# Fused two-layer transformer block on one core: x kept turned through the second half, queries and keys by column quarters, and each sample's own adapters in the linear layer

## Chip, core and metric

The kernel runs on one core of a Trainium2 chip. The metric is the device time of one launch in microseconds (us), as the median of several runs. A profiled execution gives the trace. PE is TensorE, DVE is VectorE, ACT is ScalarE, POOL is GpSimd, and SP is the queue that issues most plain DMAs.

## What is computed

64 samples of 32 tokens with 256 features, all f32, go through two layers of two residual blocks each. Several weights are picked by a per-sample index.

```python
x = x + L0_attn(L0_cond(x, idx1))       # first half
x = x + L0_ffn(L0_cond2(x, idx2))       # gated MLP with rank-16 adapters, then a ternary gated FFN
# L1_cond: H = x @ W.T;  xa = x @ A[idx3].T;  H + (xa @ B[idx3].T) * scalings[idx3]
# L1_attn: qkv = h @ W_qkv + b_qkv; 16 heads of 16; rotation of 4 of the 16; causal softmax; @ W_dense + b_dense
x = x + L1_attn(L1_cond(x, idx3))
# L1_cond2: x @ W[idx4] + b[idx4];  L1_ffn: both sides rounded to 8-bit steps, silu(gate) * up, down
x = x + L1_ffn(L1_cond2(x, idx4))
```

A and B hold 8 adapters of rank 16. W of L1_cond2 has 16 experts of 256 x 256.

## The kernel before

The 2048 tokens are eight chunks of 256 (8 samples). xq[ch] holds a chunk as two groups of 128 tokens in the partitions and 256 features in the columns. The order of instructions on each engine is the order in which the Python code lists them; nothing reorders them later.

The first half is 32 steps (4 groups of heads by 8 chunks). turn(n) mixes stages of the steps n-2 to n+1: projections and rotation (L700 on PE, L711 and L712 on DVE, L714 and L715 on POOL), scores (L810), weigh (qe, L857 on POOL), turn_qe (L871), f2 (L931 on POOL) and more. After each turn, one piece of tabulate() is listed: SP copies adapter matrices in DRAM into a layout in which one indirect gather fetches an adapter. prepare() quantizes weights of the later FFNs. load_weights brings each group's weights, load_mlp those of the second half.

The second half is turn2(n) for n from 0 to 7, and then drain(). In turn2(n), chunk n goes through gated MLP (adapters_in L401, adapters_spread L417, gate_up L436, gate_up_adapters L450, down_adapters L466, down L482), ternary FFN (ffn_up L507, ffn_down L526) and linear layer (linear_in, linear_adapters L543, linear L555 and L560). Chunk n-1 goes through attention (qkv L1098, turn_qk L1136, attn_scores L1159, attn_exp, attn_weights with the transpose L1193, attn_values L1208, attn_out L1230). Chunk n-2 goes through experts (experts_in, run_experts L1271) and the quantized FFN (turn_y, quant_up L1301, quant_h on DVE, turn_h L1325, quant_down L1341). PE works with features in the partitions for most products, so a chunk's x is turned on PE (L342, four transposes, copied out by ACT at L347) in tokens_in, linear_in and experts_in, while the residual sums are made on xq. [...]

In the linear layer before, one product with all 8 adapters side by side gives 128 rows, a mask m6 keeps the rows of each sample's own adapter, and one product with all B follows. linear_in also adds the dense bias db to xq on POOL (L537). Queries, keys and values come from one weight, qkvw, as 384 columns at a time with tokens in the partitions; turn_qk then turns queries and keys on PE in eight transposes, ACT scales the queries and DVE spreads the keys into kb.

POOL issues the indirect gathers: fetch (experts, 10 a chunk), fetch_in, fetch_out, fetch_down (adapters of the next chunk). gather copies an index column on DVE first (L366). [...] A tile is waited for where the order needs it: kb before scores, u (adapters_spread) before gate_up_adapters, h of quant_h before turn_h.

## Time and profile before

| What | Value |
|---|---|
| Median of 3 runs (lowest to highest) | 1463.49 us (1462.98 to 1463.92) |
| Profiled execution: time, span | 1462.34 us, 1460.6 us |
| Mean granted TensorE clock | 0.988 |
| First half; second half's turns; drain | to about 839; to about 1393; to 1460.6 us |
| Busy: PE, DVE, ACT, POOL | 97%, 57%, 42%, 35% of the span |

A row of the profile reads: line, engine, operation, output and inputs by the program's names, shape, count, busy us and mean ns of one, and then the idle time just before with what ended it. In a timeline the first two numbers are start and duration in us. Busy matmuls overlap, so the distance of two starts says what a step takes. An f32 matmul of the program is two records.

### The profile page before, as it was taken

How to read it: one execution, taken by the hardware profiler on the slowest of the kernel's cores; microseconds unless marked ns; L12 is line 12 of the kernel's file. 1: busy time of each engine (PE TensorE's matmuls, PEld its weight loads, DVE VectorE, ACT ScalarE, POOL GpSimd, SP SyncE). 2: the span in 40 equal slices, each digit the busy share in tenths (PEclk: the TensorE clock that was granted, in tenths of full speed). 3: DMA queues.
4: the chain of work that ended last, by engine and by line, in shares of the span. 5: the costliest groups of instructions: out<-in, count | busy, mean ns of one | idle time of the engine just before them, and what ended most of it. 6: DMA issues, size and time to landing. Idle time of an engine off the chain costs nothing.

```text
span 1460.6 us, 37036 instructions
## 1 busy us (share of the span) xinstructions
PE 1411.5 (97%) x15496; PEld 1082.4 (74%) x15496; DVE 827.1 (57%) x1899; ACT 617.0 (42%) x2014; POOL 514.4 (35%) x586
## 2 busy tenths in 40 slices
PE   5899999999999999999999999999999999999997
PEld 3666777777777777667767878788887878787865
DVE  2566677776768676667565224363636263534555
ACT  1355575656566575746566312121312121222121
POOL 3433243333424243324354243333252515152130
PEclk9999999999999999999999999999999999999999
DMA  6201010100111000100001222122221212121120
GB/s 182 55 2 66 2 30 31 34 2 12 33 39 41 9 9 12 46 2 1 13 16 50 72 79 74 52 73 59 58 75 55 78 38 84 41 73 46 43 77 18
DMA packets 61503, 65.14 MB, mean 45 GB/s; under 512 B 34901, under 2 KB 48853, under 8 KB 61337
## 3 DMA queue, kind: packets, MB, share of 16 engines
q0 software_dynamic: 13312, 35.93, 8.8%
q1 hardware_dynamic: 44824, 22.33, 5.6%
q10 hardware_dynamic: 3200, 4.52, 1.0%
q8 instruction: 122, 2.00, 0.6%
q14 instruction: 45, 0.36, 0.1%
HBM read 60.66 MB, written 3.93 MB: 44 GB/s over the span
## 4 chain that ended last, share of the span: by engine, by line
PE 92%; DMA 2%; DVE 2%; issue 2%; ACT 1%; SPq 1%; POOL 0%; DVEq 0%; POOLq 0%; ACTq 0%
PE ps L700 16%; PE ps L731 15%; PE ps L968 8%; PE ps L436 8%; PE ps L507 5%; PE ps L1301 5%; PE ps L482 3%; PE ps L1341 3%; PE ps L1098 3%; PE ps L526 3%; PE ps L913 2%; PE ps L810 2%; PE ps L450 2%; PE ps L953 2%; PE ps L888 1%
## 5 line engine op out<-in xcount | busy, mean ns | idle before, releaser
L714 POOL TENSOR_TENSOR qT<-ra,rb 128x256 f32<-128x256 f32 x64 | 46.5, 727 | 365.0 <-DVE rb L712 365.0
L922 ACT ACTIVATE sq<-ps 128x128 f32<-128x128 f32 x256 | 70.9, 277 | 213.9 <-PE ps L913 206.8
L368 POOL DMA_INDIRECT we<-in_ew,at x64 | 61.4, 960 | 255.5 <-DVE at L366 170.6
L968 PE MATMUL ps<-wo,ogT 128*128 128x256 f32 x512 | 123.3, 396 | 6.7 <-DVE aT L817 6.7
L700 PE MATMUL ps<-hsT,wq 128*128 128x256 f32 x512 | 126.5, 391 | 0.0
L700 PE MATMUL ps<-hsT,wk 128*128 128x256 f32 x512 | 121.5, 380 | 0.0
L711 DVE TENSOR_TENSOR ra<-ps,ct 128x512 f32<-128x512 f32 x128 | 87.6, 684 | 49.1 <-PE ps L700 44.1
L731 PE MATMUL ps<-wv,hsT 128*128 128x512 f32 x256 | 115.2, 593 | 0.0
L731 PE MATMUL ps<-wg,hsT 128*128 128x512 f32 x256 | 115.1, 592 | 0.0
L968 PEld LDWEIGHTS ps<-wo,ogT 128*128 128x128 f32 x512 | 97.8, 196 | 21.9 <-DVE aT L817 7.3
L700 PEld LDWEIGHTS ps<-hsT,wq 128*128 128x128 f32 x512 | 95.6, 192 | 18.3 <-issue 6.0
L794 DVE RECIPROCAL enz<-ps 128x256 f32<-128x256 f32 x64 | 107.5, 1721 | 1.5 <-PE ps L785 1.5
L700 PEld LDWEIGHTS ps<-hsT,wk 128*128 128x128 f32 x512 | 97.9, 191 | 13.4
L931 POOL TENSOR_TENSOR f<-f,mhalf 128x8 f32<-128x8 f32 x32 | 52.9, 1652 | 132.3 <-DVE f L929 132.3
L731 PEld LDWEIGHTS ps<-wg,hsT 128*128 128x128 f32 x256 | 48.7, 190 | 61.2 <-issue 54.0
L712 DVE TENSOR_TENSOR rb<-ps,ct 128x512 f32<-128x512 f32 x128 | 87.2, 681 | 0.0
L848 ACT ACTIVATE qv<-ok,nmx 128x64 f32<-128x64 f32 x256 | 84.9, 335 | 1.9 <-DVE nmx L844 1.9
L731 PEld LDWEIGHTS ps<-wv,hsT 128*128 128x128 f32 x256 | 48.6, 190 | 47.5 <-issue 45.9
L1301 PE MATMUL ps<-guT,y3T 128*128 128x352 f32 x256 | 79.6, 465 | 1.2 <-ACT y3T L347 1.2
L817 DVE SCALAR_TENSOR_TENSOR aT<-ps,ct 128x256 f32<-128x256 f32 x64 | 24.2, 419 | 86.8 <-PE ps L810 86.8
L458 DVE TENSOR_TENSOR hT<-ps,sg 128x256 f32<-128x256 f32 x64 | 24.3, 420 | 83.5 <-ACT sg L457 83.5
L507 PE MATMUL ps<-yT,f 128*128 128x256 f32 x320 | 71.2, 382 | 0.2 <-ACT yT L493 0.2
(225 smaller groups left out, 2985.3 us busy)
## 6 DMA issues: line engine op xcount, KB each, us to landing
x<-in_x SPq DMA_DIRECT2D x8, 256.0 KB, 9.4
wq<-in_wqT SPq DMA_DIRECT2D x16, 128.0 KB, 2.6
wk<-in_wkT SPq DMA_DIRECT2D x16, 128.0 KB, 3.2
wv<-in_wvT SPq DMA_DIRECT2D x4, 512.0 KB, 10.9
wg<-in_wgT SPq DMA_DIRECT2D x4, 512.0 KB, 3.9
wo<-in_woT SPq DMA_DIRECT2D x4, 512.0 KB, 4.7
row<-in_wgu ACTq DMA_DIRECT2D x11, 128.0 KB, 2.7
out<-res SPq DMA_DIRECT2D x5, 256.0 KB, 2.8
```

Source lines behind the costliest of these rows:

```text
L368: nc.gpsimd.indirect_dma_start(out=to, out_offset=None, in_=table, in_offset=bass.IndirectOffsetOnAxis(ap=at, axis=0))
L436: nc.tensor.matmul(ps[:, i * 256 : (i + 1) * 256], lhsT=mlp[name, k // 4][:, j, part], rhs=c["xT"][:, j, :], start=(i == 0 and j == 0), st ...
L507: nc.tensor.matmul(ps[:, i * 256 : (i + 1) * 256], lhsT=wt[:, j, k * P : (k + 1) * P], rhs=yT[:, j, :], start=(j == 0), stop=(j == 1),)
L700: nc.tensor.matmul(ps[:, half * 256 : (half + 1) * 256], lhsT=wt[:, c, half * 256 + pr * P : half * 256 + (pr + 1) * P], rhs=hs[:, c, lo : ...
L711: nc.vector.tensor_tensor(by_t(a.rearrange("p h t -> p (h t)")), by_t(ps), cosb, MULT)
L712: nc.vector.tensor_tensor(by_t(b.rearrange("p h t -> p (h t)")), by_t(ps), sinb, MULT)
L731: nc.tensor.matmul(ps, lhsT=hs[:, c, lo + gi * P : lo + (gi + 1) * P], rhs=wt[:, c, :], start=(c == 0), stop=(c == 1),)
L794: nc.vector.reciprocal(t[:, e, :], banks[e][:, :256])
L848: nc.scalar.activation(qv[:, k, :], ok[:, k, :], AF.Exp, bias=nmx[:, k : k + 1], accum_out=rs[:, k : k + 1],)
L922: nc.scalar.activation(sq, po[e][:, k * P : (k + 1) * P], AF.Square, accum_out=f[:, e * 4 + k : e * 4 + k + 1],)
L968: nc.tensor.matmul(ps[:, gi * D : (gi + 1) * D], lhsT=s["ogT", gi][:, h, :], rhs=w[4][:, h, :], start=(h == 0), stop=(h == 3),)
L1301: nc.tensor.matmul(ps[:, :352], lhsT=c["y3T"][:, k, gi * P : (gi + 1) * P], rhs=guT[:, k, lo : lo + 352], start=(k == 0), stop=(k == 1),)
```

## The change

x is turned once, in tokens_in, with its even and odd features as the two halves, into c["xT"], and stays so: ffn_down and attn_out add to it with features in the partitions, linear and run_experts read it, and tokens_back turns it back into xq for the last residual. A third buffer, xT3, serves every third chunk. The weights that meet xT are loaded or read with the same even and odd rows or columns. queries_keys makes queries and keys with 32 tokens of a sample as the stationary side and a quarter of the heads in each quarter of the PSUM partitions; one DVE transpose of 32 x 32 blocks turns both, the factor 0.25 moves into attn_exp, and kb is made half on ACT, half on DVE. project_values makes the values apart. In the linear layer each sample's own adapter is gathered: tabulate lists, for each chunk, eight gathers of A and one of B into a staged tile, written to own_in and own_out in DRAM; fetch_linear loads a chunk's rows. turn2 and drain are listed anew.

```diff
+        mlp["la"] = mlp["ag", 0][:, 768:].rearrange("p (j c i) -> p j c i", j=4, c=2)
+        mlp["lbt"] = mlp["ag", 1][:, 768:]
...
+alin = dram.tile([8 * P, 32], F32, tag="alin", name="alin")
+blin = dram.tile([P, D], F32, tag="blin", name="blin")
+own_in = dram.tile([8 * P, D], F32, tag="own_in", name="own_in")
+own_out = dram.tile([8 * P, D], F32, tag="own_out", name="own_out")
...
+    def staged():
+        return first.tile([P, D], F32, tag="sg", name="staged", bufs=2)
+    t = staged()
+    nc.sync.dma_start(out=t, in_=lb)
+    nc.vector.tensor_scalar(t, t, scal, None, MULT)
+    nc.sync.dma_start(out=blin, in_=t)
+    yield
+    for ch in range(8):
+        rows = slice(ch * P, (ch + 1) * P)
+        t = staged()
+        for b in range(8):
+            at = ch * 8 + b
+            gather(t[:, b * 32 : (b + 1) * 32], alin, idx("lora2", it)[:, at : at + 1], False)
+        for k in range(2):
+            nc.sync.dma_start(
+                out=own_in[rows, :].rearrange("p (j k b i) -> p k j b i", j=4, k=2, b=2)[:, k],
+                in_=t.rearrange("p (j b k i) -> p k j b i", j=4, k=2, b=2)[:, k],
+            )
+        t = staged()
+        gather(t, blin, lidx[:, ch : ch + 1], False)
+        nc.sync.dma_start(out=own_out[rows, :], in_=t)
...
 def tokens_in(ch):
     c = chunks[ch]
-    c["xT"] = turned(lambda gi, k: xq[ch][:, gi, k * P : (k + 1) * P], "xT", first, 2)
+    third = ch % 3 == 2
+    c["xT"] = turned(
+        lambda gi, k: xq[ch][:, gi, :].rearrange("p (i two) -> p two i", two=2)[:, k, :],
+        "xT3" if third else "xT", w if third else first, 1 if third else 2,
+    )
+def tokens_back(ch):
+    ps = bank()
+    for gi in range(2):
+        for k in range(2):
+            nc.tensor.transpose(
+                ps[:, gi * 256 + k * P : gi * 256 + (k + 1) * P],
+                chunks[ch]["xT"][:, k, gi * P : (gi + 1) * P], ident,
+            )
+    nc.scalar.copy(
+        xq[ch].rearrange("p g (i two) -> p g two i", two=2), ps.rearrange("p (g two i) -> p g two i", g=2, two=2)
+    )
 def gather(to, table, at, held):
...
+def fetch_linear(ch):
+    rows = slice(ch * P, (ch + 1) * P)
+    load(mlp["la"].rearrange("p j c i -> p (j c i)"), own_in[rows, :])
+    load(mlp["lbt"], own_out[rows, :])
...
     c = chunks[ch]
     ps = bank()
     for k in range(6):
-        for gi in range(2):
+        for i in range(2):
             nc.tensor.matmul(
-                ps[:, gi * D : (gi + 1) * D], lhsT=c["gT"][:, k, gi * P : (gi + 1) * P],
-                rhs=f2w[:, k, :], start=(k == 0 and gi == 0), stop=(k == 5 and gi == 1),
-            )
-    x = xq[ch].rearrange("p g f -> p (g f)")
+                ps[:, i * 256 : (i + 1) * 256], lhsT=f2w[:, k, i::2], rhs=c["gT"][:, k, :],
+                start=(k == 0 and i == 0), stop=(k == 5 and i == 1),
+            )
+    x = c["xT"].rearrange("p c t -> p (c t)")
     nc.vector.tensor_tensor(x, ps, x, ADD)
-def linear_in(ch):
-    c = chunks[ch]
-    c["xT"] = turned(lambda gi, k: xq[ch][:, gi, k * P : (k + 1) * P], "xT", first, 2)
-    nc.gpsimd.tensor_tensor(xq[ch], xq[ch], db.unsqueeze(1).to_broadcast([P, 2, D]), ADD)
 def linear_adapters(ch):
     c = chunks[ch]
     ps = bank()
     for k in range(2):
...
+        for j in range(4):
+            nc.tensor.matmul(
+                ps[32 * j : 32 * j + 32, :64], lhsT=mlp["la"][:, j, k, :],
+                rhs=c["xT"][:, k, j * 64 : (j + 1) * 64], start=(k == 0), stop=(k == 1),
+            )
+    xa = big.tile([P, 2, 2, T], F32, tag="xa", name="xa")
+    nc.vector.tensor_tensor(
+        xa, ps[:, :64].rearrange("p (b t) -> p b t", b=2).unsqueeze(1).to_broadcast([P, 2, 2, T]),
+        const("quad").rearrange("p (a b) -> p a b", a=2).unsqueeze(3).to_broadcast([P, 2, 2, T]), MULT,
+    )
+    c["xa"] = xa
+def linear(ch):
+    c = chunks[ch]
+    banks = [bank(), bank()]
+    for gi in range(2):
+        for i in range(2):
+            for k in range(2):
+                nc.tensor.matmul(
+                    banks[gi][:, i * P : (i + 1) * P], lhsT=lw[:, k, i * P : (i + 1) * P],
+                    rhs=c["xT"][:, k, gi * P : (gi + 1) * P], start=(i == 0 and k == 0), stop=False,
+                )
+    for i in range(2):
+        for gi in range(2):
+            rows = slice(64 * gi, 64 * gi + 64)
+            nc.tensor.matmul(
+                banks[gi][:, i * P : (i + 1) * P], lhsT=mlp["lbt"][rows, i * P : (i + 1) * P],
+                rhs=c["xa"][rows, :, :, :].rearrange("p a b t -> p (a b t)"), start=False, stop=(i == 1),
+            )
+    eT = big.tile([P, 2, 256], F32, tag="eT", name="eT", bufs=2)
+    for gi in range(2):
+        nc.scalar.copy(
+            eT[:, :, gi * P : (gi + 1) * P], banks[gi][:, :256].rearrange("p (c t) -> p c t", c=2)
         )
...
     c["eT"] = eT
...
+fetch_linear(0)
...
-lw = load_w("lw", [P, 2, D], lwT.rearrange("(c p) f -> p c f", p=P))
-qkvw = load_w("qkvw", [P, 2, 768], wqkv.rearrange("(c p) f -> p c f", p=P))
-qkvb = load_w("qkvb", [P, 768], bqkv.partition_broadcast(P))
+lw = load_w("lw", [P, 2, D], lwT.rearrange("(p c) f -> p c f", c=2))
+wqk = w.tile([P, 2, 4, 2, 2, 32], F32, tag="wqk", name="wqk")
+bqk = w.tile([P, 2, 2, 32], F32, tag="bqk", name="bqk")
+with nc.allow_non_contiguous_dma(reason="sixteen columns of a head"):
+    for o in range(2):
+        for which in range(2):
+            for c in range(2):
+                for i in range(4):
+                    load(
+                        wqk[:, c, i, o, which, :].rearrange("p (h d) -> p h d", h=2),
+                        wqkv[c * P : (c + 1) * P, :].rearrange(
+                            "p (o i h s d) -> p o i s h d", o=2, i=4, h=2, s=3
+                        )[:, o, i, which, :, :],
+                    )
+            for i in range(4):
+                load(
+                    bqk[32 * i : 32 * i + 32, o, which, :].rearrange("p (h d) -> p h d", h=2),
+                    bqkv.rearrange("(o i h s d) -> o i s h d", o=2, i=4, h=2, s=3)[
+                        o, i, which, :, :
+                    ].partition_broadcast(32),
+                )
+    wv = w.tile([P, 2, 16, 16], F32, tag="wv2", name="wv2")
+    for c in range(2):
+        load(wv[:, c, :, :], wqkv[c * P : (c + 1) * P, :].rearrange("p (h s d) -> p s h d", s=3, d=16)[:, 2, :, :])
+    bv = load_w("bv", [P, 16, 16], bqkv.rearrange("(h s d) -> s h d", s=3, d=16)[2, :, :].partition_broadcast(P))
...
-db = load_w("db", [P, D], bdense.partition_broadcast(P))
+db = load_w("db", [P, 2], bdense.rearrange("(p two) -> p two", two=2))
...
-def qkv(ch):
...
+def queries_keys(ch):
+    c = chunks[ch]
+    qk = work.tile([P, 2, 4, 128], F32, tag="qk", name="qk", bufs=1)
     for gi in range(2):
-        for o in range(2):
...
+        ps = bank()
+        for b in range(4):
             for k in range(2):
...
+                for i in range(4):
+                    nc.tensor.matmul(
+                        ps[32 * i : 32 * i + 32, b * P : (b + 1) * P],
+                        lhsT=c["eT"][:, k, gi * P + b * T : gi * P + (b + 1) * T],
+                        rhs=wqk[:, k, i, :, :, :].rearrange("p o s d -> p (o s d)"),
+                        start=(k == 0), stop=(k == 1),
+                    )
+        nc.vector.tensor_tensor(
+            qk[:, gi, :, :], ps.rearrange("p (b f) -> p b f", b=4),
+            bqk.rearrange("p o s d -> p (o s d)").unsqueeze(1).to_broadcast([P, 4, P]), ADD,
+        )
...
+    flat = qk.rearrange("p g b f -> p (g b f)")
+    v = flat.rearrange("p (x d) -> p x d", d=16)
...
-def turn_qk(ch):
...
+    qkT = work.tile([P, 16, 2, T], F32, tag="qkT", name="qkT", bufs=1)
+    nc.vector.transpose(qkT.rearrange("p k s t -> p (k s t)"), flat)
...
+    nc.scalar.activation(kb[:, :, 0, :], qkT[:, :, 1, :], AF.Copy, scale=const("head2")[:, 0:1])
+    nc.vector.tensor_scalar(kb[:, :, 1, :], qkT[:, :, 1, :], const("head2")[:, 1:2], None, MULT)
+    c["qkT"], c["kb"] = qkT, kb
+def project_values(ch):
+    c = chunks[ch]
+    ps = bank()
+    for gi in range(2):
+        for k in range(2):
+            nc.tensor.matmul(
+                ps[:, gi * 256 : (gi + 1) * 256], lhsT=c["eT"][:, k, gi * P : (gi + 1) * P],
+                rhs=wv[:, k, :, :].rearrange("p h d -> p (h d)"), start=(k == 0), stop=(k == 1),
+            )
     nc.vector.tensor_tensor(
...
+        vt.rearrange("p g h d -> p g (h d)"), two(ps),
+        bv.rearrange("p h d -> p (h d)").unsqueeze(1).to_broadcast([P, 2, D]), ADD,
     )
...
+        at = k // 2 * 8 + b * 2 + k % 2
...
-                lhsT=c["qT"][r, k, b * T : (b + 1) * T],
-                rhs=c["kb"][r, k * 4 + b, :, :].rearrange("p e j -> p (e j)"),
+                lhsT=c["qkT"][r, at, 0, :], rhs=c["kb"][r, at, :, :].rearrange("p e j -> p (e j)"),
...
-    nc.scalar.activation(flat, flat, AF.Exp)
+    nc.scalar.activation(flat, flat, AF.Exp, scale=0.25)
...
-    for gi in range(2):
+    for i in range(2):
         for o in range(2):
             nc.tensor.matmul(
...
+                ps[:, i * 256 : (i + 1) * 256].rearrange("p (g t) -> p g t", g=2), lhsT=dw[:, o, i::2],
+                rhs=c["aoT"][:, o::2, :, :].rearrange("p g b t -> p g (b t)"),
+                start=(i == 0 and o == 0), stop=(i == 1 and o == 1),
+            )
+    for i in range(2):
+        x = c["xT"][:, i, :]
+        nc.vector.scalar_tensor_tensor(x, ps[:, i * 256 : (i + 1) * 256], db[:, i : i + 1], x, ADD, ADD)
...
-def experts_in(ch):
...
-                    lhsT=c["x3T"][:, k, gi * P + b * T : gi * P + (b + 1) * T],
+                    lhsT=c["xT"][:, k, gi * P + b * T : gi * P + (b + 1) * T],
...
     if not begun:
         on(n, adapters_in)
-    on(n - 1, qkv)
+    on(n - 1, queries_keys)
     if not begun:
         on(n, adapters_spread)
-    gu(0, 1)
-    on(n - 1, turn_qk)
-    gu(2)
-    on(n - 2, experts_in)
-    gu(3)
-    if not begun:
-        on(n, gate_up_adapters, 0)
-    on(n - 2, run_experts)
-    for k in range(4):
-        on(n - 1, attn_scores, k)
-    gu(4)
-    on(n - 1, fetch, 0)
-    gu(5)
-    on(n - 1, attn_exp)
-    on(n - 1, fetch, 1)
-    gu(6)
-    on(n - 2, turn_y)
-    on(n - 1, fetch, 2)
-    gu(7)
-    on(n - 1, fetch, 3)
+    on(n - 1, project_values)
+    for k in range(8):
+        gu(k)
+        if k == 3:
+            if not begun:
+                on(n, gate_up_adapters, 0)
+            on(n - 2, run_experts)
+            for i in range(4):
+                on(n - 1, attn_scores, i)
+        elif k == 5:
+            on(n - 1, attn_exp)
+        elif k == 6:
+            on(n - 2, turn_y)
     if not begun:
         on(n, gate_up_adapters, 1)
     on(n - 1, attn_weights)
-    on(n - 1, fetch, 4)
+    on(n - 1, fetch, 0)
+    on(n - 1, fetch, 1)
     on(n - 2, quant_up, 0)
     on(n - 2, quant_h, 0)
-    on(n - 1, fetch, 5)
-    on(n - 1, fetch, 6)
+    on(n - 1, fetch, 2)
+    on(n - 1, fetch, 3)
     on(n, down_adapters)
     on(n + 1, fetch_in, 0)
     if not last:
...
     for b in range(1, 4):
         on(n + 1, fetch_in, b)
     on(n, down)
+    on(n - 2, tokens_back)
     on(n + 1, tokens_in)
     on(n + 1, fetch_in, 4)
-    on(n - 1, fetch, 7)
+    on(n - 1, fetch, 4)
     if not last:
         on(n - 2, turn_h, 0)
         on(n - 2, turn_h, 1)
...
         on(n - 1, attn_values, k)
     on(n, ffn_up, 0)
     on(n + 1, fetch_in, 5)
+    on(n - 1, fetch, 5)
     on(n, ffn_up, 1)
     on(n + 1, fetch_in, 6)
+    on(n - 1, fetch, 6)
     on(n, ffn_up, 2)
     on(n + 1, fetch_in, 7)
+    on(n - 1, fetch, 7)
     on(n, ffn_up, 3)
     on(n + 1, fetch_out, 0)
     on(n, ffn_up, 4)
...
         on(n - 1, attn_out)
     on(n, ffn_up, 5)
     on(n + 1, fetch_out, 2)
+    on(n - 1, fetch, 8)
+    on(n - 1, fetch, 9)
     if last:
         on(n - 2, quant_up, 1)
         on(n - 2, quant_h, 1)
+        on(n - 1, run_experts)
+        for b in range(8):
+            fetch(7, b)
     else:
         on(n - 2, quant_down, 0)
     on(n + 1, fetch_out, 3)
     on(n + 1, fetch_out, 4)
     on(n, ffn_down)
     on(n + 1, fetch_out, 5)
-    on(n - 1, fetch, 8)
-    if last:
-        on(n - 1, experts_in)
-    else:
-        on(n - 2, quant_down, 1)
     on(n + 1, fetch_out, 6)
-    on(n, linear_in)
     on(n + 1, fetch_out, 7)
     if last:
         on(n - 2, turn_h, 0)
         on(n - 2, turn_h, 1)
     else:
+        on(n - 2, quant_down, 1)
         on(n - 1, attn_out)
-    on(n - 1, fetch, 9)
     on(n, linear_adapters)
     on(n + 1, fetch_down, 0)
     on(n + 1, fetch_down, 1)
     on(n, linear)
-    if last:
-        on(n - 1, run_experts)
+    on(n + 1, fetch_linear)
 def drain():
-    qkv(7)
-    for b in range(3):
+    turn_y(6)
+    queries_keys(7)
+    quant_down(5, 0)
+    project_values(7)
+    for b in range(8, 10):
         fetch(7, b)
-    quant_down(5, 0)
-    for b in range(3, 6):
-        fetch(7, b)
-    turn_qk(7)
-    for b in range(6, 10):
-        fetch(7, b)
-    turn_y(6)
     for k in range(4):
         attn_scores(7, k)
     attn_exp(7)
...
     quant_up(6, 1)
     for k in range(4):
         attn_values(7, k)
+    quant_h(6, 0)
     quant_down(5, 1)
+    tokens_back(6)
     attn_out(7)
-    quant_h(6, 0)
-    experts_in(7)
+    turn_h(6, 0)
+    quant_down(6, 0)
     run_experts(7, (0,))
-    turn_h(6, 0)
     run_experts(7, (1,))
     quant_h(6, 1)
-    quant_down(6, 0)
+    turn_h(6, 1)
     turn_y(7, (0,))
+    quant_down(6, 1)
     quant_up(7, 0)
-    turn_h(6, 1)
     quant_h(7, 0)
     turn_y(7, (1,))
     quant_up(7, 1)
-    quant_down(6, 1)
     quant_h(7, 1)
+    tokens_back(7)
     for gi in range(2):
         turn_h(7, gi)
         quant_down(7, gi)
```

## The prediction

> **What bounds the kernel now.** I read the page's busy table first, then its chain that ended last, then the groups by shape, then the timelines of PE and DVE.
>
> ```profile
> PE 1411.5 (97%) x15496; PEld 1082.4 (74%) x15496; DVE 827.1 (57%) x1899; ACT 617.0 (42%) x2014; POOL 514.4 (35%) x586
> PE 92%; DMA 2%; DVE 2%; issue 2%; ACT 1%; SPq 1%; POOL 0%; DVEq 0%; POOLq 0%; ACTq 0%
> ```
>
> TensorE (PE) is busy for 97% of the span and is 92% of the chain. So a microsecond taken from PE's list is a microsecond of time wherever its inputs are ready, and work on other engines is free until PE has to wait for it. A busy row's duration overstates a pipelined matmul, so I price a step by the distance between starts in PE's timeline. The end of one turn of the second half (a turn lasts 77.8 us, 1002.06 to 1079.9):
>
> ```profile
> 1003.79 1.03 PE L543 MATMUL ps<-xT,ag 128*128 128x256 f32 x4
> 1004.65 1.89 PE L555 MATMUL ps<-xT,lw 128*128 128x256 f32 x8
> 1006.38 1.03 PE L560 MATMUL ps<-xa,ag 128*128 128x256 f32 x4
> 1007.34 0.46 PE L401 MATMUL ps<-xT,ag 128*32 128x32 f32 x32
> 1008.08 5.43 PE L1098 MATMUL ps<-qkvw,eT 128*128 128x384 f32 x16 [0.28 <-ACT eT L565]
> 1013.34 0.59 PE L417 MATMUL ps<-u,fold 128*128 128x256 f32 x2
> 1017.23 1.04 PE L1136 MATMUL ps<-ct,qk 128*128 128x128 f32 x8
> ```
>
> Each f32 matmul of the program is two records: 0.216 us for 256 columns (1.73 for L555's eight), 0.108 for 128. Only the drain idles much. From its DVE timeline and, last, PE's:
>
> ```profile
> 1418.05 1.71 PE L1208 MATMUL ps<-pT,vt 32*32 32x64 f32 x128 [2.60 <-DVE pT L1193]
> 1419.69 4.14 PE L1341 MATMUL ps<-dnT,h3T 128*128 128x256 f32 x12
> 1434.80 5.00 PE L1301 MATMUL ps<-guT,y3T 128*128 128x352 f32 x16 [0.46 <-ACT y3T L347]
> ```
>
> [...] behind that wait L1341's 12 records take 4.07 us, not 2.59, with a granted clock of 0.50 until about 1422. [...] L401 starts 0.96 us after L560, whose four records need 0.86, so a switch costs about 0.1 us.
>
> **The change part by part.** PE, one chunk in steady state:
>
> *Linear layer.* Gone: linear_in's 4 transposes 0.44, L543 0.86, L560 0.96, together 2.26. New: eight small adapter matmuls (16 records, 128x32 tiles, 64 columns; by L401's 14 ns a record 0.3) with two mode switches, 0.49; four 64-row adapter matmuls of 128 columns, 0.43 if two row halves overlap and 0.87 if not, taken as 0.59 plus a switch, 0.68. The main product stays (16 x 0.108). Gain 1.07.
>
> *Queries, keys, values.* Gone: L1098 5.26, the wait for eT 0.28 (two copies of half the size, the first hidden by adapters_in), turn_qk's transposes 0.87: 6.41. New: values, 4 x 256 columns, 1.73. Queries and keys: 64 matmuls of 32 stationary and 128 moving columns, four column quarters at once. No row shows that shape; run_experts has the same quarters with 256 columns (L1271: 32 records in 1.87 us, against 1.71 for perfect overlap). So 32 rounds of 0.107 are 3.41 at least; with L1271's excess and a switch 3.9; if loading weights is not hidden (L401's round, 0.058 of it, added to each), 5.3. I take 3.9. Gain 6.41 - 5.63 = 0.78, between 1.3 and -0.6.
>
> *Turns of x.* experts_in's four strided transposes (0.47) go, tokens_back's four (0.43) come: nothing. ffn_down and attn_out keep their records, with stationary columns two apart. experts_in reads its stationary so: its weight loads last 200 ns instead of 141, its step 0.47 instead of 0.44. Under 256-column matmuls that is hidden; without that cover 16 program matmuls (32 records) x 0.01 would be 0.3 a chunk.
>
> *Sum before the drain:* linear for chunks 0 to 6, 7 x 1.07 = 7.5; queries for chunks 0 to 6, 7 x 0.78 = 5.5; in the two thin turns a wait of 0.88 before x's transposes at 923.80 goes, and of 0.88 + 0.68 at 859 only 0.9 stays, since DVE writes xT directly: 1.5. **14.5 us.**
>
> *DVE and ACT behind it.* Per chunk DVE now does two 512-wide adds (0.69), the rotation (1.45 as before), a 32x32 transpose of 1024 (1.25 by L1193), half of kb (0.6; ACT the other half), before adapters_spread's u. Counted from the start of queries, u is ready at 8.8 us; gate_up_adapters needs it at 13.1. kb is ready at 8.1, needed at 15. Project_values' vt add stands behind u, at 9.5. All hidden by gate_up's 6.9 us; if they weren't, gate_up_adapters would wait. tokens_back's copy on ACT (0.58) delays aoT's by as much; sg of ffn_up waited 0.85 there, so hidden.
>
> *POOL and SP, second half.* POOL loses an add of 1.27 (L537). Four expert fetches move behind attn_weights: five microseconds of gathers (1.25 each) later in POOL's queue, in front of fetch_in and fetch_out; the last then goes out before the turn ends, and experts are needed 20 us into the next: nothing. fetch_linear's two SP loads wait for linear to finish on PE; only an out store is behind them, and nobody waits for that before the end.
>
> *First half.* In turns 5 to 12 POOL gets nine gathers after qe: 11.5 us (1.4 + 8 x 1.25, cwt's pitch). It idled there:
>
> ```profile
> 250.25 0.73 POOL L714 TENSOR_TENSOR qT<-ra,rb 128x256 f32<-128x256 f32 x1 [11.16 <-DVE rb L712]
> 256.79 1.65 POOL L931 TENSOR_TENSOR f<-f,mhalf 128x8 f32<-128x8 f32 x1 [3.43 <-DVE f L929]
> ```
>
> So qT slips by 0.4 us, and 3.4 us of idle time before L931 absorb it: nothing. Past 3.8 us in all, turn_qe on PE would wait. The own_in and own_out stores wait for gathers on SP; load_weights behind them is wanted turns later. Extra index operations on DVE in turn 1: 0.6 at most. Zero taken, 0 to 4 us lost.
>
> *Weights at the seam.* One load of qkvw becomes 48 small ones and three of 64-byte pieces, on SP after 834.5.
>
> ```profile
> L269 SPq DMA_DIRECT2D qkvw<-in_wqkv x1: 460/460/460, 834.9 to 834.9; - x1
> L315 SPq DMA_DIRECT2D alora<-in_ad x8: 545/664/1942, 44.6 to 275.4; - x8
> ```
>
> SP spent 0.46 us on qkvw, 0.66 on 1024 pieces (0.92 each in a row of six). From 835.2, 48 x 0.46 end at 857.3, landed by 860; queries_keys(0) comes at about 863. At 0.66 they'd land at 869: a wait of 6. The value weights (4096 pieces, some 3.7 us) land near 864, wanted at 867. I take no stall, bound 0 to 8 with a cold clock.
>
> *Drain and turn 7.* run_experts(6) moves ahead of ffn_down(7); its 3.9 us of DVE work now delay x's add, so PE waits 0.9 before linear_adapters(7). Still the lighter PE list and the lost wait for kb (0.97) bring attn_values(7) from 1418.05 to about 1414.7: 3.4 gained. Then it turns: turn_h(6,1) is now listed ahead of quant_up(7,0), and needs quant_h(6,1), which DVE does behind both halves of run_experts(7). Before, quant_up(7,0) lay over that. From DVE's timeline: half an expert 2.29 (1429.25 to 1431.54), twice, then 2.98 (1433.82 to 1436.80) less the second half's matmuls 0.95: PE idles **6.8 us**, and 1.7 more at half clock. Before, quant_down(6,0), turn_y and 0.5 of waiting stood there. Waits after attn_values come to 9.1 instead of 4.3; with the cold clock and tokens_back the tail is 6.4 longer. Drain: 3.0 lost (0 to 6).
>
> **Sum:** 14.5 - 3.0 = 11.5 us. The profiled execution has a span of 1460.6 and a time of 1462.34; the median of 1463.49 is 1.15 above it, so I subtract from the median: **1452.0**, span about 1449.1.
>
> **Rivals.**
> 1. *Cheaper than priced:* quarters overlap perfectly (4.0 more), and the tail costs nothing (3.0): 1445. For it L1271's 9% loss; against it that the DVE order in the drain is fixed by the list.
> 2. *Weights late at the seam:* 6 us of waiting and 2 of cold clock: 1460. For it the 0.92 us of SP per load of pieces; against it their smaller size, 256 pieces each.
> 3. *Slower: the quarters overlap badly.* L401's round at 32 columns shows weight loads, not columns. If only two of four overlap, queries_keys costs 6.9 instead of 3.9: 8 x 3.0 = 24 lost, 1476. It decides from 5.3 us a chunk (42 ns a record), where 1.4 x 8 eats the gain. Against it L1271's 58 ns for twice the columns.
> 4. *POOL late in the first half:* at 2.0 us a gather nine take 18.4, 3.4 beyond the slack, 8 turns: 27 lost, 1479. Against it the steady 1.25.
> 5. *The edit isn't felt:* PE finds other waits as long as what it sheds. PE's idle time in a steady turn, 0.3 us, speaks against it.
>
> **How the numbers follow.** Forecast 0.60, rival 1 0.16, rival 2 0.10, rival 3 0.07, rival 4 0.05, rival 5 0.02. What a measurement here can tell from no change is about 0.2%, 2.9 us. Faster takes the forecast, rival 1 and half of rival 2: 0.81; same the other half and rival 5: 0.07; slower rivals 3 and 4: 0.12. The forecast alone spans 1447 to 1457; with rival 1 and most of rival 2 the range is 1444.5 to 1460.
>
> **What would show it.** Right: queries_keys' matmuls near 3.9 us a chunk, a steady turn near 76 us, no PE wait over 1 us from 100 to 860 us and before queries_keys(0), and one PE wait of 6 to 7 us for quant_h in the drain with a granted clock of half after it. Wrong: queries_keys above 5 us; PE waiting for wqk or wv from DMA near 863; turn_qe waiting for POOL in turns 6 to 13; no long wait in the drain.

## The result, and the profile after

The changed kernel takes 1451.24 us (median of 4, 1450.69 to 1451.58), the kernel before 1463.34 beside it: ratio 0.9917, 95% interval 0.9899 to 0.9934. The profiled execution has a span of 1449.7 us against 1460.6, so 10.9 us to account for. The forecast was 1452.0 and a span of 1449.1.

The experiments ran later, on four chips (numbers 3, 5, 7 and 8). In all but e11_drain_only (chip 5), PE waited again and again inside its steps, mostly in runs of small matmuls, for what the trace calls "issue": time in which the engine waits for nothing that the profile shows. There the kernel before took 1549 to 1551 us and the changed kernel (after_again) 1654. Totals are compared within these runs only, and even there e1 to e4 ran on chip 3, after_again, best, e5 and e8 on chip 7, e9 and e10 on chip 8, so a few us of a total decide nothing.

The page of after, busy time and the chain that ended last:

```profile
PE 1399.7 (97%) x16552; PEld 1086.2 (75%) x16552; DVE 829.9 (57%) x1879; ACT 614.1 (42%) x2014; POOL 577.2 (40%) x650
PE 91%; DMA 3%; SPq 2%; DVE 2%; issue 1%; ACT 1%; POOL 0%; ACTq 0%; DVEq 0%
```

PE executes 1056 more records and is busy 11.8 us less: the new ones are small and overlap. PE is still the bound. The end of a steady turn in PE's timeline (start, duration, line, work):

```profile
998.18 0.43 PE L611 MATMUL ps<-xT,ag 128*32 128x64 f32 x16
998.54 2.05 PE L629 MATMUL ps<-xT,lw 128*128 128x128 f32 x16
1000.52 0.72 PE L636 MATMUL ps<-xa,ag 64*128 64x128 f32 x8
1001.17 0.46 PE L472 MATMUL ps<-xT,ag 128*32 128x32 f32 x32
1001.70 3.70 PE L1206 MATMUL ps<-wqk,eT 128*32 128x128 f32 x128
1005.33 0.70 PE L488 MATMUL ps<-u,fold 128*128 128x256 f32 x2
1005.86 1.89 PE L1242 MATMUL ps<-wv,eT 128*128 128x256 f32 x8
1007.59 1.03 PE L507 MATMUL ps<-xT,cgt 128*128 128x256 f32 x4
```

From start to start, the linear layer takes 2.99 us (998.18 to 1001.17), and with the gap ahead of L611 3.08; before it took 3.55, and 0.44 for linear_in. Queries and keys take 3.63, the values 1.73. From adapters_in to gate_up it is 6.42 us; before it was 6.43 and 0.87 for turn_qk. A steady turn lasts 76.27 us (998.54 to 1303.63, four turns) instead of 77.79.

PE's waits in the second half (us in total, times, longest), and the drain in its timeline:

```profile
PE ps L1422 <- DVE h L204: 7.0, 1, 7.0
PE ps L1310 <- DVE pT L1295: 2.6, 1, 2.6
PE ps L537 <- DVE hT L529: 2.2, 2, 1.9
PE ps L1438 <- ACT h3T L1425: 1.5, 3, 0.5
PE ps L611 <- issue: 0.8, 1, 0.8
```

```profile
1401.47 1.91 PE L1310 MATMUL ps<-pT,vt 32*32 32x64 f32 x128 [2.58 <-DVE pT L1295]
1403.30 3.71 PE L1438 MATMUL ps<-dnT,h3T 128*128 128x256 f32 x12
...
1413.08 1.93 PE L1368 MATMUL ps<-we,xT 128*32 128x256 f32 x32
1422.00 1.09 PE L1422 MATMUL ps<-ct,h 128*128 128x128 f32 x4 [6.98 <-DVE h L204]
...
1423.76 3.71 PE L1438 MATMUL ps<-dnT,h3T 128*128 128x256 f32 x12
...
1443.49 2.86 PE L1438 MATMUL ps<-dnT,h3T 128*128 128x256 f32 x12 [0.46 <-ACT h3T L1425]
```

attn_values(7) (L1310) starts 16.6 us earlier than before, the last matmul group ends 10.7 earlier: the tail between them has grown from 39.0 to 44.9 us. In it stands the wait for quant_h(6,1), 6.98 us, and the matmuls behind it run at half clock (granted clock 0.50 from 1420 to 1425 us): from 1422.00 to 1427.31 they take 5.31 us. At full clock it would be 3.57: eight transposes at 0.108 each, 0.87, and 2.70 for the twelve records of L1438, as later in the drain.

The first half ends as before: ffn_up(0) starts at 843.76 us, before at 843.72. But this is a sum of opposites. The changed kernel is 2.9 us late at its first L1047 (101.42 against 98.56; e11_drain_only, the same up to there, 99.56) and 3.6 late at 600 us. Then it wins 3.7 us in two steps, around this wait (before, after):

```profile
625.02 6.38 PE L968 MATMUL ps<-wo,ogT 128*128 128x256 f32 x16 [3.45 <-DVE aT L817]
627.59 3.72 PE L1047 MATMUL ps<-wo,ogT 128*128 128x256 f32 x16 [2.40 <-DVE aT L896]
```

Ahead of aT, VectorE rounds a weight row whose load it waits for, 6.37 us before and 5.33 after; and behind the shorter wait PE kept its full clock (granted clock 1.00 from 626.81 to 630.23 us; in before 0.50 from 623.61 to 630.43). The gathers themselves cost little: over turns 5 to 12 the changed kernel loses 0.4 us. The page's group of POOL's qT shows where the nine gathers a turn went, into idle time (busy, mean ns, then idle before):

```profile
L793 POOL TENSOR_TENSOR qT<-ra,rb 128x256 f32<-128x256 f32 x64 | 46.6, 728 | 272.6 <-DVE rb L791 272.5
```

It was 365.0 before. At the seam, SP's loads (ns least/median/longest, first and last start) end as PE arrives:

```profile
L276 SPq DMA_DIRECT2D wqk<-in_wqkv x32: 368/467/1295, 835.7 to 859.3; - x32
L276 SPq DMA_DIRECT2D bqk<-in_bqkv x16: 425/427/488, 841.0 to 861.4; - x16
L276 SPq DMA_DIRECT2D wv<-in_wqkv x2: 556/960/1365, 861.8 to 862.4; - x2
```

queries_keys(0) starts at 863.04 and takes 3.94 instead of 3.63, the values 2.12 instead of 1.73: 0.7 us more. For the values the trace names the weights: PE's weight load waits 0.53 us for wv. For queries_keys(0) it names only eT (0.18), so those 0.3 us aren't shown to come from the loads.

### The profile page after: what moved, and what is told of

Its sections match the earlier page's. It is cut to its first block, busy times and chain, and to the rows that moved or that the text cites. A ratio compares the mean times of both kernels' runs of the same rounds, so it can differ in the third digit from the quotient of the medians.

```text
span 1449.7 us, 39390 instructions
## 1 busy us (share of the span) xinstructions
PE 1399.7 (97%) x16552; PEld 1086.2 (75%) x16552; DVE 829.9 (57%) x1879; ACT 614.1 (42%) x2014; POOL 577.2 (40%) x650
## 4 chain that ended last, share of the span: by engine, by line
PE 91%; DMA 3%; SPq 2%; DVE 2%; issue 1%; ACT 1%; POOL 0%; ACTq 0%; DVEq 0%
PE ps L779 16%; PE ps L810 15%; PE ps L1047 8%; PE ps L507 8%; PE ps L1398 5%; PE ps L578 4%; PE ps L553 3%; PE ps L1438 3%; PE ps L597 3%; PE ps L992 2%; PE ps L521 2%; PE ps L889 2%; PE ps L1206 2%; PE ps L1032 2%; SPq L276 1%; PE ps L967 1%
## 5 line engine op out<-in xcount | busy, mean ns | idle before, releaser
L1047 PE MATMUL ps<-wo,ogT 128*128 128x256 f32 x512 | 120.6, 389 | 6.1 <-DVE aT L896 6.1
L790 DVE TENSOR_TENSOR ra<-ps,ct 128x512 f32<-128x512 f32 x128 | 87.4, 683 | 49.9 <-PE ps L779 44.9
L1047 PEld LDWEIGHTS ps<-wo,ogT 128*128 128x128 f32 x512 | 95.8, 192 | 20.9 <-DVE aT L896 6.6
L433 POOL DMA_INDIRECT ag<-alora,at x56 | 53.4, 954 | 49.3 <-DVE at L431 39.3
```

Source lines behind the costliest of these rows:

```text
L433: nc.gpsimd.indirect_dma_start(out=to, out_offset=None, in_=table, in_offset=bass.IndirectOffsetOnAxis(ap=at, axis=0))
L790: nc.vector.tensor_tensor(by_t(a.rearrange("p h t -> p (h t)")), by_t(ps), cosb, MULT)
L1047: nc.tensor.matmul(ps[:, gi * D : (gi + 1) * D], lhsT=s["ogT", gi][:, h, :], rhs=w[4][:, h, :], start=(h == 0), stop=(h == 3),)
```

## The experiments

### The drain: e1_drain, best, e11_drain_only

```diff
 # e1_drain
-        turn_h(6, 1)
         turn_y(7, (0,))
-        quant_down(6, 1)
         quant_up(7, 0)
+        turn_h(6, 1)
+        quant_down(6, 1)
```

> The changed kernel with two lines of the drain moved: turn_h(6,1) and quant_down(6,1) are listed behind quant_up(7,0) instead of ahead of it. Theory (the listing costs the wait): turn_y(7,0) can start when y's first half is done, at about 1416.5, so quant_up(7,0) lies over quant_h(6,1) on VectorE; the wait of 6.98 us becomes one of about 1.5 ahead of turn_y(7,0) and 0.5 for y3T, and quant_down(6,1) runs at full clock (2.6 us instead of 3.6). quant_up(7,1) then starts near 1427.5 instead of 1432.9: about 5 us less, 1446 (1444.5 to 1448). Rival 1 (the wait only moves): VectorE's order is unchanged, PE waits as long in front of quant_up(7,1) or of the last turn_h: within 1 us of 1451. Rival 2 (the clock is what costs, not the wait): a wait over 2.5 us stays and with it the half clock: only 1 to 2 us less, 1449.5.

Its time was 1645.74 us, 8.0 less than after_again's 1653.76 on another chip, so the stretch has to tell. From attn_out(7)'s start to the end of the last matmul it takes 35.1 us; after takes 39.1 (after_again 39.0), the kernel before 33.4. So 3.9 us less, within the expected range. (The 5.2 that best's expectation gives for this stretch is the distance from attn_values(7), 44.9 against 39.7.) The wait for quant_h is gone, but the half clock is not: behind a wait of 1.72 us and one of 0.46, quant_up(7,0) takes 6.53 us to the next start instead of 4.84, with a granted clock of 0.58 from 1616 to 1618 us. PE's timeline of e1_drain:

```profile
1614.50 0.41 PE L390 MATMUL ps<-ct,y 128*128 128x128 f32 x2 [1.72 <-DVE y L204]
1615.37 6.69 PE L1398 MATMUL ps<-guT,y3T 128*128 128x352 f32 x16 [0.46 <-ACT y3T L395]
1621.90 0.60 PE L1422 MATMUL ps<-ct,h 128*128 128x128 f32 x4
```

So the listing was the cause, as rival 1 there denied, and the clock is a second cost that such a wait can bring. The next kernel fills the 1.72 us too.

```diff
 # drain of best and e11_drain_only (best also loads bqk behind the value weights)
         turn_h(6, 0)
-        quant_down(6, 0)
         run_experts(7, (0,))
         run_experts(7, (1,))
+        quant_down(6, 0)
         quant_h(6, 1)
-        turn_h(6, 1)
         turn_y(7, (0,))
-        quant_down(6, 1)
         quant_up(7, 0)
-        quant_h(7, 0)
         turn_y(7, (1,))
+        turn_h(6, 1)
+        quant_h(7, 0)
         quant_up(7, 1)
+        quant_down(6, 1)
         quant_h(7, 1)
```

> The changed kernel with the drain listed anew once more (quant_down(6,0) between run_experts(7) and turn_y(7,0); turn_h(6,1) behind quant_up(7,0); quant_down(6,1) behind quant_up(7,1)), and at the seam the 16 loads of bqk issued behind those of the value weights. Theory: PE has 2.6 us of quant_down(6,0) over VectorE's first half of y and 4.9 us of quant_up(7,0) over quant_h(6,1), so neither the wait of 6.98 us nor the half clock behind it is left: about 8.5 us less in the drain (e1_drain's single move gave 5.2 from attn_out(7) to the end); value weights land by 861, wanted at 867: 0.7 less at the seam. 1442 (1440.5 to 1444) where after takes 1451. Rival (VectorE is the bound of the drain by then: quant_h(7,1) is late for turn_h(7,1)): 4 to 6 less, 1446. Rival at the seam: bqk, issued last, is late for the add of queries_keys(0), and what is gained at values is lost at scores: nothing there.

> The changed kernel with the drain as in best and nothing else: the loads at the seam stay as in after. Theory: from attn_out(7) to the end it takes 29.7 us as in best, where after takes 39.0: 9.4 less than after, whatever the first 1400 us take: 1644 where after takes 1654, 1442 where it takes 1451. If the seam's order brought part of best's 11.5 us: best beats this kernel by 1 to 2 us. If the two are equal to 1 us, the order of bqk and the value weights is worth nothing here.

best took 1642.25 us, 11.5 less than after_again on the same chip. e11_drain_only came where PE has none of these "issue" waits: 1439.83 us (4 runs) beside 1460.52 for the kernel before, ratio 0.987 (0.9837 to 0.9903). PE's timeline of e11_drain_only from quant_down(6,0) on:

```profile
1409.18 2.86 PE L1438 MATMUL ps<-dnT,h3T 128*128 128x256 f32 x12
1411.87 0.38 PE L390 MATMUL ps<-ct,y 128*128 128x128 f32 x2
1412.72 5.00 PE L1398 MATMUL ps<-guT,y3T 128*128 128x352 f32 x16 [0.46 <-ACT y3T L395]
...
1418.43 4.97 PE L1398 MATMUL ps<-guT,y3T 128*128 128x352 f32 x16
1423.24 2.75 PE L1438 MATMUL ps<-dnT,h3T 128*128 128x256 f32 x12
...
1431.59 2.86 PE L1438 MATMUL ps<-dnT,h3T 128*128 128x256 f32 x12 [0.46 <-ACT h3T L1425]
```

From here on no wait is over 0.53 us, and attn_out(7) to the end is 29.66 us, in best as well: 9.4 less than after, as expected. The order of VectorE's work was not the bound. Whether best's order of loads at the seam brings anything stays open: best and e11 didn't run in the same conditions, and best's seam had other waits. At the seam of e11_drain_only, which keeps after's loads, PE does wait for the value weights, longer than in after:

```profile
867.54 1.56 PE L1242 MATMUL ps<-wv,eT 128*128 128x256 f32 x6 [1.18 <-DMA wv<-in_wqkv]
```

### The column quarters: e4_quarters, e8_runs

```diff
 # e4_quarters
             for b in range(4):
-                for k in range(2):
-                    for i in range(4):
+                for i in range(4):
+                    for k in range(2):
 # e8_runs
-            for b in range(4):
-                for k in range(2):
-                    for i in range(4):
+            for i in range(4):
+                for b in range(4):
+                    for k in range(2):
```

> The changed kernel with the loop over the four column quarters put outside the loop over the two halves of the features, in queries_keys alone: the same 64 matmuls a chunk, but two matmuls on the same quarter follow each other. Theory (matmuls on different quarters overlap when they follow each other, which the listing order gives): pairs on one quarter cannot overlap, so about half of the fourfold overlap goes: between 5 and 7.5 us a chunk instead of 3.63, 11 to 31 us more in all. If the engine overlaps across the queue whatever the order: 3.7 us, no change. [...]

> The changed kernel with the loop over the four column quarters outermost in queries_keys, so that eight matmuls (16 records) on one quarter follow each other, where e4_quarters had two (4 records) and its queries_keys took as long as after's (records of 273 ns at the same pitch). [...] between 7 and 13.8 us a chunk instead of 3.63, 27 to 81 us more. If the order never matters: within 1 us of after.

e4_quarters took 1656.34 us, 2.6 more than after_again on another chip, with overlapping ranges, so the total tells nothing. Its least disturbed chunks take 3.70 us for queries and keys, as after_again's (3.64 to 3.67): four records in a row on one quarter still overlap with the others. e8_runs, sixteen in a row, took 1706.78, 53 more; an undisturbed chunk in its PE timeline:

```profile
1444.36 11.74 PE L1206 MATMUL ps<-wqk,eT 128*32 128x128 f32 x128
1456.04 0.70 PE L488 MATMUL ps<-u,fold 128*128 128x256 f32 x2
```

11.68 us, 91 ns a record instead of 28; 128 records of 0.108 us one after the other would take 13.8. So the quarters do run beside each other, as long as the listing brings another quarter within a few records: within four it does, sixteen are too many. By what means they overlap isn't in the traces. This is what the forecast's rival 3 would have looked like: 8.0 us more a chunk, past the 5.3 us a chunk from which that rival decides. The changed kernel's order keeps clear of it.

### One part undone: e2_qkv_old, e3_linear_old

```diff
 # e2_qkv_old: qkv, turn_qk, attn_scores and the loads of qkvw, qkvb as in the kernel before
-        on(n - 1, queries_keys)
+        on(n - 1, qkv)
...
-        on(n - 1, project_values)
...
+            if k == 1:
+                on(n - 1, turn_qk)
```

> The changed kernel with queries, keys and values made as before the change: token-major product of 768 columns, rotation, eight transposes on PE, one load of the weights; everything else as changed. Theory (the prediction's step, as the trace of after corrects it): a chunk loses 0.88 us of PE from adapters_in's start to gate_up's, seven or eight times, and the seam wins back some 0.7: 6 us more, 1457 (1455.5 to 1459). By the prediction's own 0.78 a chunk: 5.5 more. Rival (the gain of the second half comes from x kept turned, and the quarters only trade PE time for waits): at most 2 us more, 1453. Rival (VectorE's transpose costs more than the trace of PE tells): faster than after.

The total, 1651.19 us, is 2.6 less than after_again. Its sign is that of the last rival, but the runs are of two chips, their ranges overlap (1648.35 to 1653.88 and 1652.51 to 1658.81), and PE's "issue" waits, 6.4 us at queries_keys alone in after_again, are larger than the difference, so the total doesn't decide. An undisturbed chunk does: from adapters_in to gate_up 6.22 us, and 0.87 for turn_qk's transposes, 7.09 against after's 6.42. So queries, keys and values by the new way are worth 0.67 us a chunk. The other 0.21 of the 0.88 seen between before and after is a shorter step from adapters_in to the product (0.53 instead of 0.74): eT is copied in halves, and that belongs to the linear layer's two banks.

```diff
 # e3_linear_old: all adapters and the mask m6 as in the kernel before; no own_in, own_out, fetch_linear
-    mlp["la"] = mlp["ag", 0][:, 768:].rearrange("p (j c i) -> p j c i", j=4, c=2)
+    mlp["la"] = load(mlp["ag", 0][:, 768:]..., laT.rearrange("(p c) f -> p c f", c=2))
...
-                    rhs=c["xa"][rows, :, :, :].rearrange("p a b t -> p (a b t)"), start=False, stop=(i == 1),
+                    rhs=c["xa"][:, gi * P : (gi + 1) * P], start=False, stop=(i == 1),
```

> The changed kernel with the linear layer's adapters as before: all adapters for all tokens and a mask, no tables of own adapters in the first half, no fetch_linear; x stays turned and the main product stays split by groups of tokens. Theory 1 (the prediction's sizes: 0.86 to 0.49 and 0.96 to 0.68): 0.65 us more a chunk, 5 us more in all, 1456.5. Theory 2 (the trace of after, where the linear layer takes 3.08 us and the split main product 1.98 of it, not 1.73): about 0.4 more a chunk, 3 us in all, 1454.5 (1453.5 to 1455.5). Rival (switches and the small tiles eat the gain): within 1 us of 1451.2. In the first half nothing changes with the gathers gone if they lay in POOL's idle time: ffn_up(0) starts at 843.8 as before.

In PE's timeline an undisturbed linear layer takes 3.63 us (0.86 for the first adapters, 1.79, 0.98) against 3.08 with its gap: own adapters are worth 0.55 us a chunk, between the two theories. The main product takes 1.79 behind 128-wide tiles and 1.98 behind the small ones, so about 0.2 us of their gain goes into that step. But the total was 1555.07, 99 us less than after_again, where the theories had expected 3 to 5 us more and the rival no change. Of the 99 us, 94 lie in steps 5 to 12 of the first half, in which after_again gathers the adapters.

### Gathers beside small matmuls: after_again, before_again, e5_pool6, e9_spread

> The changed kernel itself once more, as the reference of this series. [...] 0.9917 of the kernel before, 1451. If PE waits inside its runs of small matmuls for nothing that the profile shows ('issue'), as it did in the series of e1_drain: longer than the kernel before, because the changed kernel has 1056 more matmul records and more gathers beside them; then totals of this series tell nothing of the parts, and the parts are read from stretches without such waits.

> The kernel before, for its trace in this series: 1550. Theory (the stalls of this chip fall on runs of small matmuls that lie beside gathers): the first half is free of them, since nothing is gathered in turns 5 to 12; the 87 us over 1463 lie in the second half, at scores, attn_values and the adapters, where gathers run. Rival (PE's clock is lower throughout): the granted clock is below 0.99 in quiet stretches, and large matmuls take longer.

after_again took 1653.76 us, ratio to before 1.0676 (1.0652 to 1.07): where PE has these waits, the change makes the kernel slower. PE's timeline of after_again in a step with nine gathers on POOL:

```profile
267.89 1.00 PE L889 MATMUL ps<-qT,kT 64*64 64x64 f32 x40
269.29 0.37 PE L889 MATMUL ps<-qT,kT 64*64 64x64 f32 x5 [0.40 <-issue]
270.06 0.33 PE L889 MATMUL ps<-qT,kT 64*64 64x64 f32 x4 [0.41 <-issue]
...
274.44 0.48 PE L889 MATMUL ps<-qT,kT 64*64 64x64 f32 x4 [0.99 <-issue]
...
279.84 6.33 PE L1047 MATMUL ps<-wo,ogT 128*128 128x256 f32 x16
```

scores and what follows it to L1047 take 12.0 us instead of 1.8, while POOL's gathers run, and L1047 behind it takes 6.33 us instead of 3.72, as long as before's L968 at a granted clock of 0.50 (6.38). Eight such steps last 282.2 us, by the starts of qe (L936), where before_again's same steps last 187.6: 94 us. What PE waits for there isn't in the trace. From 265 to 278 us its DMA view has one transfer of instructions (0.02 MB) beside those of POOL's gathers and SP's stores; after's view of the same stage has two (0.03 MB), and there PE doesn't wait. So late instructions aren't shown to be the cause.

before_again, 1551.64 us, has none of it between 200 and 490 us, as expected. But of the 90 us by which its span is longer than before's, 23 lie ahead of ffn_up(0), against the expectation: 8 at the start, and 15 in the last steps of the first half, where four gathers of chunk 0's adapters lie over scores (PE, then POOL):

```profile
782.50 0.80 PE L810 MATMUL ps<-qT,kT 64*64 64x64 f32 x18 [1.10 <-issue]
776.79 1.05 POOL L368 DMA_INDIRECT ag<-alora,aidx  x1 [0.17 <-issue]
780.64 0.94 POOL L368 DMA_INDIRECT bx<-blora,bidx  x1 [0.30 <-issue]
```

The other 67 us lie in the second half, where PE's "issue" waits are 16.4 us at attn_values, 8.8 at gate_up_adapters and 8.3 at scores, and the granted clock of a stretch of 100 us falls to between 0.88 and 0.98; undisturbed large matmuls keep their length (1.73 us for the main product). So the first theory held, small matmuls beside gathers, in more places than it named; the rival of a lower clock throughout did not.

```diff
 # e5_pool6, ahead of the gather from blin
+            for b in range(6):
+                at = ch * 8 + b
+                gather(t[:, b * 32 : (b + 1) * 32], alin, idx("lora2", it)[:, at : at + 1], False)
```

> The changed kernel with six more gathers in each of the eight turns that build own_in (15 instead of 9 of 1.25 us; they fetch again what is there). The prediction's slack: POOL idled 11.16 and 3.43 us a turn, nine gathers take 11.5, so 3.1 us are left and 7.5 are added: 4.4 us a turn late at turn_qe on PE, 35 us more in all, 1486. If POOL is late where the small matmuls of PE can go on without it (more slack than two rows show): under 8 us more. If each gather also holds up other DMA: over 45 more.

1674.08 us, 20.3 more than after_again, which none of the three forecasts gave (35, under 8, over 45); a step with 15 gathers lasts 38.3 us instead of 35.3. PE's waits between 195 and 500 us are still "issue" ones, nearly all at scores (L892 there) and attend (L913), none for POOL. So this run says nothing on POOL's slack of 3.1 us: another limit came first.

```diff
 # e9_spread (with e11's drain): own_tables yields after each gather
             on(n + 1, project_qk, "k", 0)
+            if n >= 5:
+                next(own, None)
+                next(own, None)
...
                 next(tabulating, None)
+            if n >= 5:
+                next(own, None)
```

> The changed kernel with the drain as in best (the loads at the seam as in after) and the 72 gathers of own_in and own_out spread: three a turn over 24 turns instead of nine a turn over eight, two of them behind kT of column pair 0 (POOL idles 3.4 us there, PE multiplies 128 x 512 tiles) and one behind qe, so that none lies over the 64x64 matmuls of scores (L889). Theory (on this chip nine gathers behind qe hold up PE's instructions in scores: with them a turn lasts 35.1 us, without them, in e3_linear_old, 23.4): turns 5 to 12 fall back to 23.4 to 24 us each, about 90 us less than best, 1550 (1545 to 1560). Rival 1 (the stall goes with the number of gathers, wherever they are): no gain, 1640. Rival 2 (POOL is late: 3 x 1.25 in an idle time of 3.4 us delays qe and turn_qe on PE): 0.3 to 0.5 us a turn, 8 to 12 us on top of 1550.

1553.38 us: 89 less than best (on another chip, where the kernel before took as long, 1551), with the same instructions but for their place (and the order of bqk at the seam). PE's timeline and POOL's of e9_spread, same stage:

```profile
244.47 1.16 PE L894 MATMUL ps<-qT,kT 64*64 64x64 f32 x64
245.45 0.92 PE L972 MATMUL ps<-qeT,es 64*64 64x64 f32 x32
246.29 3.72 PE L1052 MATMUL ps<-wo,ogT 128*128 128x256 f32 x16
```

```profile
256.56 0.96 POOL L438 DMA_INDIRECT staged<-alin,it  x1
257.83 0.95 POOL L438 DMA_INDIRECT staged<-alin,it  x1 [0.30 <-issue]
259.86 1.68 POOL L1015 TENSOR_TENSOR f<-f,mhalf 128x8 f32<-128x8 f32 x1 [1.08 <-DVE f L1013]
```

The step is back at 23.3 us, and the two gathers fit the 3.43 us in which POOL idled before f, of which 1.08 are left. So it isn't the total number of gathers that holds PE up, but their lying over runs of 64x64 matmuls. That three gathers a step are simply too few is no way out: in before_again four a step, lying over scores, cost 3.4 to 5.9 us. Rival 2 (POOL late) did not come either.

### Both gains: e10_masked_drain

e3_linear_old's linear layer with e11's drain.

> e3_linear_old (masked adapters in the linear layer, no tables of own adapters) with the drain as in best. Theory: both gains add, since they lie 550 us apart: 1555 less the 9.4 us that best's drain is shorter between attn_out(7) and the end: 1545.5 (1543 to 1548), less than the kernel before (1551) on this chip. [...] Rival (the chip's stalls change with the drain): over 1550.

1544.27 us, ratio to before 0.9963 (0.9946 to 0.998), as the theory's sum had it. It beats both kernels where PE has these "issue" waits (the kernel before by 0.4%), as e11_drain_only (1439.83) does where it has none; e10 was not run in quiet conditions.

## Why the prediction was right

| Step | Predicted | Measured |
|---|---|---|
| Linear layer, a chunk | 1.07 gained | 0.91 gained |
| Queries, keys, values, a chunk | 0.78 gained | 0.88 gained |
| Steady turn, by the two steps | 1.85 less, "near 76" | 1.52 less, 76.27 |
| First half | 0 | 0.04 lost (3.6 lost, then 3.7 gained, 0.1 lost) |
| Seam | 0 | 0.7 lost |
| Up to attn_values(7) | 14.5 + 3.4 = 17.9 gained | 16.6 gained |
| Tail of the drain | 6.4 lost | 5.9 lost |
| Sum | 11.5 | 10.7 to the last matmul, 10.9 of span |

**The sum is better than its terms.** Against the 17.9 up to attn_values(7), about 1.1 us were missed at the linear layers, 1.6 at attn_values and 0.7 at the seam, while queries and keys brought 0.7 more. Two more gains close the gap: the wait ahead of linear_adapters(7) was 0.7 us shorter than forecast, and in chunk 1's turn the down step behind a wait of 1.9 us took 8.39 us instead of 9.07, since the half clock lasted 3.4 us there and not 6.8 (granted clock 0.50 from 893.06 to 896.47 us, in before from 893.26 to 900.09). Nobody forecast the last one, nor the two opposite amounts in the first half. The steps were priced soundly; that the sum came within 1 us is in part luck.

**Bound.** PE stayed the bound (97%, 91% of the chain), so counting PE's list was the right method.

**Linear layer.** The two adapter steps were well priced: 0.45 with the gap, not 0.49, and 0.65, not 0.68. What the forecast calls a switch is a change of tile shape; its 0.1 us was an estimate from the one step of L560 (128x128 tiles) to L401 (128x32). In after the gap ahead of L611, at the same change, is 0.09 us. The mis-sized term is the main product, priced as unchanged at 1.73 (16 x 0.108): behind small tiles it takes 1.98. e3_linear_old, where it takes 1.79, bears the extra 0.2 out. (The forecast's own terms, 2.26 less 0.49 and 0.68, give 1.09, not 1.07.)

**Queries and keys.** 3.63 us against 3.9 taken and 3.41 as the perfect case; 28 ns a record. L1271, the row of the same quarters with 256 columns, was the right neighbour to price by. The four column quarters run together, 3.8 times faster than 128 records of 0.108 us one after the other, and e8_runs adds that the list must change the group often enough: four records in a row on one do no harm, sixteen do.

**The missing 0.27 us a turn.** The two steps gain 1.79, the turn 1.52. attn_values takes 2.17 us in after and 1.91 before, in chunks 1 to 5, 1.85 against 1.61 in chunk 0, and the same in chunk 6 (1.91 and 1.89). The forecast had this step unchanged. tokens_back ahead of it can't be the reason, since chunk 0 has none there. POOL's gathers lie beside this step in both kernels and keep POOL about as long (1.70 and 1.62 us in chunk 4); the cause is open.

**DVE and ACT behind PE: nothing; POOL and SP in the second half: nothing.** Right: no wait on kb, u or the gathers stands in the table of waits.

**First half: nothing.** Right for the gathers in the quiet runs: 0.4 us, with their 11.5 us a turn taken from idle time. That the half as a whole came out at 0.04 is luck, as shown above. The sign "no PE wait over 1 us from 100 to 860 us" was badly set: after has waits of 2.73 and 2.40 us for aT in that stretch, but before has them too, 2.52 and 3.45. The bound of 0 to 4 us and rival 4's 27 looked at POOL alone. Elsewhere the same gathers cost 94 us, by "issue" waits of PE that the trace of before doesn't show and that no rival named.

**Seam.** The 48 loads were priced at 22.1 us (48 x 0.46) and take 26.1 (835.7 to 861.8): 0.54 each from start to start, the longest 1.30. So the value weights landed at 868, not at 864, and the margin of 3 us was nil. The sign that was to show the forecast wrong, PE waiting for wv, did come: the mechanism of rival 2 exists, but it cost 0.4 us in after (0.7 with what isn't explained) and a wait of 1.18 in e11_drain_only, not 8.

**Drain.** The wait was forecast as 6.8 (its terms, twice 2.29 and 2.98 less 0.95, add up to 6.6) and is 6.98, the half clock behind it as 1.7 and is 1.7 (5.31 less 3.57); e1_drain shows that the listing makes them. The wait of 0.9 before linear_adapters(7) was 0.2. For before's L1341 behind its wait the forecast gives 4.07 us; from start to start it is 3.98.

## What to carry to other kernels

Price a step by the distance of starts, and take a new shape's price from the nearest row that uses the engine in the same way. When an order is listed by hand, look at each wait that the new order makes for work that could lie over it: here 9.4 us, nearly as much as the whole change, lay in the order of a few lines of the drain. Keep gathers away from long runs of small matmuls, even where both engines seem to have time: the same ones cost 0.4 us in after and 94 in after_again. When a sum of many terms comes out right, compare it stage by stage: here the zero of the first half was 3.7 us lost and 3.7 won.

## What the runs showed of the hardware

- PE can stop inside runs of small matmuls for nothing that the profile shows ("issue"): in after_again 0.2 to 1.6 us after each 1 to 5 records of 64x64 tiles while POOL gathers (from 200 to 580 us 52.0 us in 80 such waits), in after, with the same instructions and gathers, not once from 200 to 840 us. In after_again's second half 12 such stops (6.3 us) lie at quant_down too, whose tiles are 128x128 (L1438). Why some chips or times show it isn't settled; what PE waits for isn't in the trace.
- A wait's length alone doesn't set the half clock. Behind PE's wait for pT in the drain, quant_down's twelve records take 3.98 us in before (wait of 2.60 us), 3.55 in after (2.58) and 4.84 in best (2.99), but 2.70 in e11_drain_only (2.58) and in after_again (2.98). In the traces of before and after each stretch at a granted clock of 0.50 that ends inside the span lasts 3.41 or 6.83 us and starts a whole number of 3.41 us behind the one ahead of it (in after 893.06 to 896.47, 1401.64 to 1405.06, 1418.71 to 1425.54). With the span divided into steps of 3.41 us at these edges, from 100 us on, PE idled 1.63 us or more in the step ahead of each such stretch (1.63 from 889.85 in before, 2.55 from 1415.50; 2.58 from 1398.23 in after) and at most 1.70 in a step that full clock followed (from 623.40 in after). What sets these steps isn't in the traces.
- Matmuls on one column quarter, four records in a row (e4_quarters), still overlap with those of other quarters; sixteen (e8_runs) hardly do (29 against 91 ns a record, where no overlap would be 108).
